# Self attention of a Perceiver layer: the two heads of a pair on row halves and column halves of TensorE, and the division moved ahead of the turn

## The chip, the cores and the metric

The kernel runs on one core of one Trainium2 chip. The metric is the device time of one execution in microseconds; the time before is the median of three runs, 806.36 us (806.20 to 808.21). All arithmetic is float32.

## The reference

One Perceiver layer for 256 query tokens of width 512. First comes a sigmoid cross attention over a context of 25088 rows, then self attention with 16 heads of width 64 that share one key and one value, then a mixture-of-experts feed-forward. The change touches the self attention alone:

```python
xn = layernorm(x)
q  = xn @ w_q.T                       # 16 heads of 64
k, v = split(xn @ w_kv.T)             # one key and one value, 64 wide, for all heads
sim  = (q * scale) @ k.T              # per head, 256 x 256, causal mask
attn = softmax(sim)                   # max, exp, sum, divide
out  = attn @ v                       # per head, 256 x 64
out  = layernorm(concat(out) @ w_out.T) * lno_g + lno_b
x    = x + out
```

## The kernel before

The 256 tokens stand as `NT` = 2 tiles of 128 (t = 0, 1); the 16 heads as `NE` = 8 pairs e, so that one pair has 128 channels, 64 of each head. The kernel goes through three stages in turn: the cross attention (49 groups of the context, about 560 us), the self attention, and the feed-forward. In the self attention nothing is loaded that isn't there yet; it is work of TensorE, VectorE, ScalarE and, in the new version, GpSimd, all of which run their instructions in order.

Before the pairs, `head_keys` and `head_values` make the shared key and value, and `queries(e)` (line 617) makes a pair's queries with four products of 256 columns. The key is kept in `kd` twice: rows 0 to 63 hold it in the first half of the columns, rows 64 to 127 in the second half, and the rest is zero. So one product with the full height of 128 rows (line 704) yields the scores of both heads of a tile t: 2 x 128 columns for t = 0 and 2 x 256 for t = 1, half of it multiplied by zeros.

For each tile t of a pair, `probabilities` adds the causal mask to the diagonal block (VectorE, line 707), takes the negated row maximum (line 709) and exponentiates head by head on ScalarE (line 712). `turned` transposes the probabilities on TensorE (line 727), six blocks of 128 x 128 per pair, and evicts them as `pT`. `weighted` multiplies each turned block as the stationary operand with `va` (line 751): the value with a column of ones as the 65th, so that the row sum comes out beside the weighted values. It divides with a reciprocal and a product on VectorE (lines 761 and 763). `outputs` turns the result (line 771) and evicts it to `oT` (line 777), from which `project` (line 677) makes the output, 2 x 8 products of 512 columns that add up in two PSUM banks.

The loop over e is a pipeline written by hand: in step e stand the queries of pair e+1, the turn of pair e-1, the scores of pair e, the values of pair e-1 and the outputs of pair e-2. Most of the pairs' instructions are placed by the scheduler from that order; the last pairs and everything marked `in_turn` stay as written. `fill` puts six of the projections between the last steps. PSUM has eight banks: six that rotate through `bank()`, so that the scores of consecutive tiles and pairs lie in different banks, and two that gather the projection.

Of the kernel before, what the change touches and what calls it, by code (L numbers as in the profile page):

```python
# [9 lines left out]
F32 = mybir.dt.float32  # L10
AF = mybir.ActivationFunctionType
ALU = mybir.AluOpType
AX = mybir.AxisListType

P = 128
# [6 lines left out]
def tile_perceiver_layer(  # L22
# [25 lines left out]
    nc = tc.nc  # L48

    T, D = x.shape  # L50
# [3 lines left out]
    DH = a_wkvT.shape[1] // 2  # L54
# [4 lines left out]
    NT = T // P  # L59
# [4 lines left out]
    NE = INNER // P  # L64
# [5 lines left out]
    small = ctx.enter_context(tc.tile_pool(name="small", bufs=4))  # L70
# [4 lines left out]
    psum = cross.enter_context(tc.tile_pool(name="psum", bufs=4, space=bass.MemoryType.PSUM))  # L75
    pacc = cross.enter_context(tc.tile_pool(name="pacc", bufs=4, space=bass.MemoryType.PSUM))

    def bank(name):
        return psum.tile([P, 512], F32, tag="ps", name=name)
# [72 lines left out]
    def all_of(src):  # L152
# [33 lines left out]
    ident = const.tile([P, P], F32, tag="ident", name="ident")  # L186
# [22 lines left out]
    tri = const.tile([P, 2, P], F32, tag="tri", name="tri")  # L209
# [6 lines left out]
        fill=NEG,  # L216
# [18 lines left out]
    in_turn = tc.keep_in_program_order  # L235
# [158 lines left out]
    sums, channel_sums = {}, {}  # L394
# [61 lines left out]
    for c in range(ND):  # L456
# [3 lines left out]
                lhsT=wqT_sb[:, c, :],  # L460
                rhs=xnT[:, c, :],
                start=(c == 0),
                stop=(c == ND - 1),
# [39 lines left out]
    for t in range(NT):  # L503
        for j in range(J):
# [4 lines left out]
                    rhs=ones_sb,  # L509
# [31 lines left out]
        layernorm(an[:, t, :], x1[:, t, :], f"a{t}", twice=True)  # L541

    cross.close()
    psum = ctx.enter_context(tc.tile_pool(name="psum_b", bufs=6, space=bass.MemoryType.PSUM))
    pacc = ctx.enter_context(tc.tile_pool(name="pacc_b", bufs=2, space=bass.MemoryType.PSUM))

# [54 lines left out]
    aq = hpool.tile([P, NE, T], F32, tag="aq", name="aq")  # L603
    oT = hpool.tile([P, NE, T], F32, tag="oT", name="oT")

    kd = hpool.tile([P, 2, T], F32, tag="kd", name="kd")
    nc.gpsimd.memset(kd, 0.0)

    va = hpool.tile([P, NT, DH + 1], F32, tag="va", name="va")
    nc.gpsimd.memset(va, 1.0)  # L610

    def queries(e, lo=0, hi=T, mark=lambda ins: ins):

        pa = bank(f"pa_{e}_{lo}")
        for c in range(ND):
            mark(
                nc.tensor.matmul(  # L617
                    pa[:, 0 : hi - lo],
                    lhsT=a_wqT_sb[:, c, e * P : (e + 1) * P],
                    rhs=anT[:, c, lo:hi],  # L620
                    start=(c == 0),
                    stop=(c == ND - 1),
                )
            )
        mark(
            nc.vector.tensor_scalar(aq[:, e, lo:hi], pa[:, 0 : hi - lo], 1.0 / DH, None, ALU.mult)
        )

    def head_keys(lo, hi):
        pkk = bank(f"pkk_{lo}")  # L630
        for c in range(ND):
            in_turn(
                nc.tensor.matmul(
                    pkk[:, 0 : hi - lo],
                    lhsT=a_wkv_sb[:, c, 0:2, :].rearrange("p i d -> p (i d)"),
                    rhs=anT[:, c, lo:hi],
                    start=(c == 0),
                    stop=(c == ND - 1),
                )
            )  # L640
        for i in range(2):
            nc.scalar.copy(
                kd[i * DH : (i + 1) * DH, i, lo:hi], pkk[i * DH : (i + 1) * DH, 0 : hi - lo]
            )

    def head_values(t):
        pv = bank(f"pv_{t}")
        for c in range(ND):
            in_turn(
                nc.tensor.matmul(  # L650
                    pv[:, :DH],
                    lhsT=anT[:, c, t * P : (t + 1) * P],
                    rhs=a_wkv_sb[:, c, 2, :],
                    start=(c == 0),
                    stop=(c == ND - 1),
                )
            )
        in_turn(nc.vector.tensor_copy(va[:, t, :DH], pv[:, :DH]))

    head_keys(0, P)  # L660
    queries(0, 0, P, in_turn)
# [13 lines left out]
    def project(t, e):  # L675
        in_turn(
            nc.tensor.matmul(  # L677
                pw[t],
                lhsT=oT[:, e, t * P : (t + 1) * P],
                rhs=a_wout_sb[:, e, :],  # L680
                start=(e == 0),
                stop=(e == NE - 1),
            )
        )

    fillers = [(0, e) for e in range(NE - 2)]

    def fill(e, n):
        for _ in range(n if e == NE - 1 else 0):
            project(*fillers.pop(0))  # L690

    def at_end(e, ins):
        if e >= NE - 1:
            in_turn(ins)

    def probabilities(e):

        found = []
        for t in range(NT):
            nk = (t + 1) * P  # L700
            nm = f"{e}_{t}"
            ps = bank(f"ps_{nm}")
            sc = ps[:, : 2 * nk].rearrange("p (i k) -> p i k", i=2)
            nc.tensor.matmul(  # L704
                sc, lhsT=aq[:, e, t * P : (t + 1) * P], rhs=kd[:, :, 0:nk], start=True, stop=True
            )
            nc.vector.tensor_add(sc[:, :, t * P : nk], sc[:, :, t * P : nk], tri)
            nmx = small.tile([P, 2], F32, tag="nmx", name=f"nmx_{nm}")
            nc.vector.tensor_reduce(nmx, sc, AX.X, ALU.max, negate=True)
            pe = work_b.tile([P, 2, nk], F32, tag=f"pe{t}", name=f"pe_{nm}")  # L710
            for i in range(2):
                nc.scalar.activation(pe[:, i, :], sc[:, i, :], AF.Exp, bias=nmx[:, i : i + 1])
            found.append(pe)
        return found

    def turned(e, found):

        done = []
        for t, pe in enumerate(found):
            fill(e, 2 - t)  # L720
            pt = bank(f"ptp_{e}_{t}")
            for kt in range(t + 1):
                for i in range(2):
                    o = (2 * kt + i) * P
                    at_end(
                        e,
                        nc.tensor.transpose(  # L727
                            pt[:, o : o + P], pe[:, i, kt * P : (kt + 1) * P], ident
                        ),
                    )  # L730
            n = 2 * (t + 1) * P
            pT = work_b.tile([P, n], F32, tag=f"pT{t}", name=f"pT_{e}_{t}")
            if t == 0:
                nc.scalar.copy(pT, pt[:, :n])
            else:
                nc.vector.tensor_copy(pT, pt[:, :n])
            done.append(pT)
        return done

    def weighted(e, done):  # L740

        fill(e, 2)
        po = bank(f"po_{e}")
        ov = po[:, : 2 * NT * (DH + 1)].rearrange("p (t i d) -> p t i d", t=NT, i=2)
        for t, pT in enumerate(done):
            for i in range(2):
                for kt in range(t + 1):
                    o = (2 * kt + i) * P
                    at_end(
                        e,  # L750
                        nc.tensor.matmul(  # L751
                            ov[:, t, i, :],
                            lhsT=pT[:, o : o + P],
                            rhs=va[:, kt, :],
                            start=(kt == 0),
                            stop=(kt == t),
                        ),
                    )
        rs = small.tile([P, NT * 2, 1], F32, tag="rsm", name=f"rsm_{e}")
        flat = ov.rearrange("p t i d -> p (t i) d")  # L760
        nc.vector.reciprocal(rs, flat[:, :, DH : DH + 1])
        on = work_b.tile([P, NT * 2, DH], F32, tag="oh", name=f"oh_{e}")
        nc.vector.tensor_mul(on, flat[:, :, 0:DH], rs.to_broadcast([P, NT * 2, DH]))
        return on

    def outputs(e, on):
        pt = bank(f"pto_{e}")
        for t in range(NT):
            at_end(
                e + 1,  # L770
                nc.tensor.transpose(
                    pt[:, t * P : (t + 1) * P],
                    on[:, 2 * t : 2 * t + 2, :].rearrange("p i d -> p (i d)"),
                    ident,
                ),
            )
        nc.scalar.copy(oT[:, e, :], pt[:, :T])

    found, heads = {}, {}
    for e in range(NE + 2):  # L780
        if e + 1 < NE:
            queries(e + 1)
        done = turned(e - 1, found.pop(e - 1)) if e - 1 in found else None
        if e < NE:
            found[e] = probabilities(e)
        if done is not None:
            heads[e - 1] = weighted(e - 1, done)
        if e - 2 in heads:
            if e == NE + 1:
                fill(NE - 1, len(fillers))  # L790
            outputs(e - 2, heads.pop(e - 2))


    fn = work.tile([P, NT, D], F32, tag="tok", name="fn")
# [16 lines left out]
        )  # L811
        layernorm(fn[:, t, :], x2[:, t, :], f"f{t}")

    project(0, NE - 2)
    project(1, 0)
    project(0, NE - 1)
    attended(0)
    for e in range(1, NE):
# [2 lines left out]
    attended(1)  # L821

    heads_end.close()
    few = ctx.enter_context(tc.tile_pool(name="few", bufs=1))


# [487 lines left out]
```

## Time and profile before

| What | Value |
|---|---|
| Median of 3 runs | 806.36 us (806.20 to 808.21) |
| The profiled execution: its own time, its span | 807.88 us, 805.8 us |
| Granted TensorE clock, mean over the span | 0.996 |
| Busy share: TensorE products (PE) | 98% |
| VectorE (DVE), ScalarE (ACT), GpSimd (POOL) | 62%, 13%, 1% |
| First product of scores, pair 0 | 586.08 us |
| First product of scores, pair 7 | 619.81 us |
| First transposition after the projection (`pt_fn`) | 639.07 us |
| Between the first and the last of these: busy TensorE, VectorE, ScalarE | 52.08, 30.65, 19.20 of 52.99 us |

Times inside the execution count from the start of the span. A float32 product is two matmul records in the trace (a transposition is one), and the columns that stream set its time: the 256-column records follow one another at 0.21 us, the 512-column ones at 0.43 us. The end of a record lies about 0.17 us behind the start of the one that follows, since the array is a pipeline. PE is TensorE's products, PEld its weight loads.

### The profile page before, as it was taken

The page shows a single profiled execution, that of the slowest core. Times are in us where ns is not written, and L with a number is a line of the kernel's source. Part 1 is how long each engine was busy: PE and PEld are TensorE (multiplying, and loading weights), DVE is VectorE, ACT ScalarE, POOL GpSimd, SP SyncE. Part 2 cuts the span into 40 slices and gives each one's busy share as a digit, 9 for nine tenths or more (in the row PEclk, how much of TensorE's full clock was granted, in tenths as well). Part 3 has the DMA queues.
Part 4 walks back from the last instruction along what each step waited for, and adds up shares of the span by engine and source line. Part 5 has one row for each costly group of instructions (what it writes and reads, how often), then busy time and mean ns, then how long its engine had stood idle before and what let it go on. Part 6 is the DMA issues. An engine that isn't in the chain of part 4 may idle for free.

```text
span 805.8 us, 8698 instructions
## 1 busy us (share of the span) xinstructions
PE 792.4 (98%) x3326; PEld 576.6 (72%) x3326; DVE 500.9 (62%) x828; ACT 108.6 (13%) x209; POOL 6.9 (1%) x28
## 2 busy tenths in 40 slices
PE   8999999999999999999999999999999999999996
PEld 5777777777777777777777777777687676776563
DVE  5766777667776677766777667776466563512212
ACT  2111110111001110011100111001234220110110
POOL 1000000000000000000000000000100000000000
PEclk9999999999999999999999999999999999999999
DMA  9997999999999888998889988810700032669500
GB/s 253 244 196 182 258 232 267 239 222 222 218 210 204 188 187 169 194 201 189 184 171 194 201 187 186 166 44 0 235 1 1 1 129 81 240 234 389 180 1 30
DMA packets 150495, 139.58 MB, mean 173 GB/s; under 512 B 7984, under 2 KB 109872, under 8 KB 150448
## 3 DMA queue, kind: packets, MB, share of 16 engines
q1 hardware_dynamic: 150160, 138.96, 73.0%
q8 instruction: 28, 0.46, 0.3%
q14 instruction: 19, 0.16, 0.1%
q10 hardware_dynamic: 288, 0.00, 0.0%
HBM read 138.42 MB, written 0.52 MB: 172 GB/s over the span
## 4 chain that ended last, share of the span: by engine, by line
PE 97%; DVE 1%; DMA 0%; ACT 0%; issue 0%; POOL 0%; POOLq 0%
PE xacc L439 37%; PE pk L338 21%; PE pz L360 11%; PE ph_e L873 7%; PE pd_e L919 3%; PE ph_s L873 3%; PE pa L617 2%; PE pw L677 2%; PE pd_s L919 2%; PE ph_few L1141 1%; PE ps L704 1%; PE po L751 1%; PE ph_first L873 1%; PE po_few L1172 1%; PE ptp L727 1%; PE py L530 1%
## 5 line engine op out<-in xcount | busy, mean ns | idle before, releaser
L338 PE MATMUL pk<-cT,wkT_sb 128*128 128x512 f32 x376 | 169.0, 592 | 0.0
L439 PE MATMUL xacc<-T,S 128*128 128x256 f32 x588 | 134.9, 379 | 0.0
L368 ACT ACTIVATE zT<-pz 128x512 f32<-128x512 f32 x98 | 58.3, 597 | 479.9 <-PE pz L360 479.2
L439 PEld LDWEIGHTS xacc<-T,S 128*128 128x128 f32 x588 | 111.7, 190 | 15.2
L338 PEld LDWEIGHTS pk<-cT,wkT_sb 128*128 128x128 f32 x376 | 71.4, 190 | 69.9 <-issue 67.4
L309 DVE STREAM_TRANSPOSE cT<-quarters 128x2048 f32<-128x2048 f32 x47 | 108.3, 2304 | 0.0
L439 PEld LDWEIGHTS xacc<-ctx,zT 128*128 128x128 f32 x392 | 74.3, 190 | 31.3 <-issue 23.0
L439 PE MATMUL xacc<-ctx,zT 128*128 128x256 f32 x392 | 93.0, 380 | 0.1
L360 PE MATMUL pz<-qT,kT 128*128 128x256 f32 x392 | 92.6, 379 | 0.0
L360 PEld LDWEIGHTS pz<-qT,kT 128*128 128x128 f32 x392 | 74.4, 190 | 10.1
L407 DVE TENSOR_TENSOR S<-zT 128x256 f32<-128x256 f32 x49 | 20.8, 425 | 91.5 <-ACT zT L368 91.5
L347 DVE TENSOR_SCALAR kT<-pk,bk 128x512 f32<-128x512 f32 x49 | 36.8, 750 | 59.8 <-PE pk L338 59.8
L873 PE MATMUL ph_e<-fT,gu 128*128 128x256 f32 x256 | 57.2, 381 | 0.0
L380 DVE TENSOR_TENSOR zsum<-zsum,zT 128x1024 f32<-128x1024 f32 x48 | 56.8, 1183 | 0.0
L873 PEld LDWEIGHTS ph_e<-fT,gu 128*128 128x128 f32 x256 | 48.1, 190 | 10.6 <-issue 3.8
L439 PE MATMUL xacc<-ctx,S 128*128 128x256 f32 x196 | 50.3, 379 | 0.0
L439 PE MATMUL xacc<-T,zT 128*128 128x256 f32 x196 | 50.3, 379 | 0.0
L439 PEld LDWEIGHTS xacc<-ctx,S 128*128 128x128 f32 x196 | 37.2, 190 | 5.1
L439 PEld LDWEIGHTS xacc<-T,zT 128*128 128x128 f32 x196 | 37.2, 190 | 5.1
L418 DVE TENSOR_TENSOR T<-ctx,T 128x512 f32<-128x512 f32 x49 | 33.9, 692 | 1.7
L419 DVE TENSOR_TENSOR T<-ctx 128x512 f32<-128x512 f32 x49 | 33.5, 685 | 0.0
L420 DVE TENSOR_TENSOR T<-T,ctx 128x512 f32<-128x512 f32 x49 | 33.5, 684 | 0.0
(228 smaller groups left out, 618.2 us busy)
## 6 DMA issues: line engine op xcount, KB each, us to landing
ctx<-in_context SPq DMA_DIRECT2D x48, 1024.0 KB, 6.9
quarters<-in_context SPq DMA_DIRECT2D x188, 256.0 KB, 9.2
gu<-in_e_gate_up SPq DMA_DIRECT2D x12, 1024.0 KB, 7.7
dn<-in_e_down SPq DMA_DIRECT2D x11, 512.0 KB, 6.2
gu_s<-in_s_gate_up SPq DMA_DIRECT2D x8, 512.0 KB, 5.9
a_wqT<-in_a_wqT SPq DMA_DIRECT2D x1, 2048.0 KB, 9.1
a_wout<-in_a_woutT SPq DMA_DIRECT2D x1, 2048.0 KB, 8.9
dn_s<-in_s_down SPq DMA_DIRECT2D x4, 512.0 KB, 7.6
```

The lines of the kernel that those rows point to most:

```text
L309: in_turn(nc.vector.transpose(cT, q.rearrange("p b (c r) -> p c b r", r=R)))
L338: nc.tensor.matmul(pk, lhsT=w[:, c, :], rhs=cT[:, c, :, :].rearrange("p b r -> p (b r)"), start=(c == 0), stop=(c == ND - 1),)
L347: in_turn(nc.vector.tensor_scalar(kT, pk, bk_sb, None, ALU.add))
L360: nc.tensor.matmul(pz[:, i * T : (i + 1) * T], lhsT=kT[:, j * P : (j + 1) * P], rhs=qT, start=True, stop=True,)
L368: nc.scalar.activation(zT[:, 2 * h : 2 * h + 2, :].rearrange("p j t -> p (j t)"), pz, AF.Sigmoid, scale=1.0 / math.sqrt(QK),)
L380: in_turn(nc.vector.tensor_add(zsum, zsum, zT))
L418: in_turn(nc.vector.tensor_sub(t2, c_of(ct, 1, 1), t1))
L419: in_turn(nc.vector.tensor_sub(t3, c_of(ct, 1, 1), c_of(ct, 0, 1)))
L420: in_turn(nc.vector.tensor_sub(t4, t2, c_of(ct, 1, 0)))
L439: nc.tensor.matmul(product[nm], lhsT=lhs[:, p, :], rhs=rhs[:, p, :], start=(g == 0 and p == 0 and nm in ("00", "2", "1", "11")), stop=(g = ...
L873: nc.tensor.matmul(ph[:, f * T + lo : f * T + hi], lhsT=gu[:, c, col : col + P], rhs=fT[:, c, lo:hi], start=(c == 0), stop=(c == ND - 1),)
L919: nc.tensor.matmul(pd, lhsT=hT[:, f, t * P : (t + 1) * P], rhs=dn[:, f, :], start=(f == 0), stop=(f == NI - 1),)
```

## The change

The scores: instead of one full-height product per tile, each head has its own product over 64 rows, head 0 on rows 0 to 63 and head 1 on rows 64 to 127, written to different PSUM banks. The tile of scores is now one object of two banks, `ps2`, with a single buffer (`bufs=1`): both tiles t of a pair lie in it, and the next pair's scores use it again. The rotating pool shrinks from six banks to four.

The softmax: the row sums come from the exponential itself (`accum_out`) instead of the column of ones. `divided` takes the reciprocal on VectorE and multiplies the probabilities on GpSimd, before they are turned. The turn of pair e-2 stands in step e now (it was pair e-1).

The values: the value is the stationary operand (128 rows x 64 columns) and the turned probabilities stream; head 0 writes PSUM partitions 0 to 63 and head 1 partitions 64 to 127. The result comes out turned already, so `outputs` with its transposition goes away, and so do the division on VectorE and the zeroed and doubled key `kd`.

The queries are evicted by ScalarE instead of VectorE, and one of the two turned blocks is evicted by the other engine than before. All instructions of the pairs now stay in program order.

```diff
-    psum = ctx.enter_context(tc.tile_pool(name="psum_b", bufs=6, space=bass.MemoryType.PSUM))
+    psum = heads_psum.enter_context(
+        tc.tile_pool(name="psum_b", bufs=4, space=bass.MemoryType.PSUM)
...
-        mark(
-            nc.vector.tensor_scalar(aq[:, e, lo:hi], pa[:, 0 : hi - lo], 1.0 / DH, None, ALU.mult)
+        in_turn(
+            nc.scalar.activation(aq[:, e, lo:hi], pa[:, 0 : hi - lo], AF.Copy, scale=1.0 / DH)
...
+    def scored(e):
+        ps = psum.tile([P, 2, 512], F32, tag="ps2", name=f"ps_{e}", bufs=1)
+        parts, maxima = [], []
+        for t in range(NT):
+            nk = (t + 1) * P
+            lo = t * P
+            parts.append(ps[:, :, lo : lo + nk])
+            for i in range(2):
+                half = slice(i * DH, (i + 1) * DH)
+                in_turn(nc.tensor.matmul(ps[:, i, lo : lo + nk],
+                        lhsT=aq[half, e, t * P : (t + 1) * P],
+                        rhs=kk[half, 0:nk], start=True, stop=True))
+        for t, sc in enumerate(parts):
+            diagonal = sc[:, :, t * P : (t + 1) * P]
+            in_turn(nc.vector.tensor_add(diagonal, diagonal, tri))
+            nmx = small.tile([P, 2], F32, tag="nmx", name=f"nmx_{e}_{t}")
+            in_turn(nc.vector.tensor_reduce(nmx, sc, AX.X, ALU.max, negate=True))
+            maxima.append(nmx)
+        return parts, maxima, []
+
+    def exponential(e, t):
...
+        for i in range(2):
+            in_turn(nc.scalar.activation(
+                    pe[:, i, :], parts[t][:, i, :], AF.Exp, bias=maxima[t][:, i : i + 1],
+                    accum_out=sums[:, i, :]))
+
+    def divided(e, t):
+        pe, sums = scores_of[e][2][t]
+        rs = small.tile([P, 2, 1], F32, tag="rsm", name=f"rsm_{e}_{t}")
+        in_turn(nc.vector.reciprocal(rs, sums))
+        nc.gpsimd.tensor_mul(pe, pe, rs.to_broadcast([P, 2, (t + 1) * P]))
...
+    def weighted(e, done):
+        po = bank(f"po_{e}")
+        for kt, pT in enumerate(done):
+            for i in range(2):
+                in_turn(nc.tensor.matmul(po[i * DH : (i + 1) * DH, kt * P : T],
+                        lhsT=va[:, kt, :], rhs=pT[:, i, :],
+                        start=(kt == 0), stop=(kt == NT - 1)))
+        in_turn(nc.scalar.copy(oT[:, e, :], po[:, :T]))
...
+    for e in range(NE + 2):
+        done = None
+        if e >= NE:
+            fill(2)
+        if e - 1 in scores_of:
+            divided(e - 1, 0)
+        if e - 2 in scores_of:
+            done = turned(e - 2)
+        if e - 1 in scores_of:
+            divided(e - 1, 1)
+        if e + 1 < NE:
+            queries(e + 1, mark=in_turn)
+        if e < NE:
+            scores_of[e] = scored(e)
+            exponential(e, 0)
+        else:
+            fill(1)
+        if done is not None:
+            weighted(e - 2, done)
+        if e < NE:
+            exponential(e, 1)
```

More of the change, by code (lines that the diff above doesn't have):

```diff
@@ L543, in tile_perceiver_layer @@
     cross.close()
-    psum = ctx.enter_context(tc.tile_pool(name="psum_b", bufs=6, space=bass.MemoryType.PSUM))
     pacc = ctx.enter_context(tc.tile_pool(name="pacc_b", bufs=2, space=bass.MemoryType.PSUM))
+    heads_psum = ExitStack()
+    psum = heads_psum.enter_context(
+        tc.tile_pool(name="psum_b", bufs=4, space=bass.MemoryType.PSUM)
+    )
     NS = IS // I
@@ L604, in tile_perceiver_layer @@
     oT = hpool.tile([P, NE, T], F32, tag="oT", name="oT")
[L606 to L610, printed above, removed]
+    kk = hpool.tile([P, T], F32, tag="kk", name="kk")
+    va = hpool.tile([P, NT, DH], F32, tag="va", name="va")
     def queries(e, lo=0, hi=T, mark=lambda ins: ins):
@@ L640, in head_keys @@
             )
[L641 to L644, printed above, removed]
+        nc.scalar.copy(kk[:, lo:hi], pkk[:, 0 : hi - lo])
     def head_values(t):
@@ L657, in head_values @@
             )
-        in_turn(nc.vector.tensor_copy(va[:, t, :DH], pv[:, :DH]))
+        in_turn(nc.vector.tensor_copy(va[:, t, :], pv[:, :DH]))
     head_keys(0, P)
@@ L684, in project, with fill @@
         )
-    fillers = [(0, e) for e in range(NE - 2)]
-    def fill(e, n):
-        for _ in range(n if e == NE - 1 else 0):
+    fillers = [(0, e) for e in range(NE - 1)] + [(1, 0)]
+    def fill(n):
+        for _ in range(n):
             project(*fillers.pop(0))
[L692 to L698, printed above, removed]
+    def scored(e):
+        ps = psum.tile([P, 2, 512], F32, tag="ps2", name=f"ps_{e}", bufs=1)
+        parts, maxima = [], []
@@ L699, in probabilities @@
         for t in range(NT):
             nk = (t + 1) * P
[L701 to L705, printed above, removed]
-            )
-            nc.vector.tensor_add(sc[:, :, t * P : nk], sc[:, :, t * P : nk], tri)
-            nmx = small.tile([P, 2], F32, tag="nmx", name=f"nmx_{nm}")
-            nc.vector.tensor_reduce(nmx, sc, AX.X, ALU.max, negate=True)
@@ L710, in probabilities @@
-            pe = work_b.tile([P, 2, nk], F32, tag=f"pe{t}", name=f"pe_{nm}")
-            for i in range(2):
[L712 to L726, printed above, removed]
+            lo = t * P
@@ new lines, in scored @@
+            parts.append(ps[:, :, lo : lo + nk])
+            for i in range(2):
+                half = slice(i * DH, (i + 1) * DH)
+                in_turn(
+                    nc.tensor.matmul(
+                        ps[:, i, lo : lo + nk],
+                        lhsT=aq[half, e, t * P : (t + 1) * P],
+                        rhs=kk[half, 0:nk],
+                        start=True,
+                        stop=True,
+                    )
+                )
+        for t, sc in enumerate(parts):
[4 more added lines that the diff above has]
+            maxima.append(nmx)
@@ new lines, in scored @@
+        return parts, maxima, []
+    def exponential(e, t):
+        parts, maxima, found = scores_of[e]
+        nm = f"{e}_{t}"
+        pe = work_b.tile([P, 2, (t + 1) * P], F32, tag=f"pe{t}", name=f"pe_{nm}", bufs=3)
+        sums = small.tile([P, 2, 1], F32, tag="sums", name=f"sums_{nm}")
+        for i in range(2):
+            in_turn(
+                nc.scalar.activation(
+                    pe[:, i, :], parts[t][:, i, :], AF.Exp, bias=maxima[t][:, i : i + 1],
+                    accum_out=sums[:, i, :],
+                )
+            )
+        found.append((pe, sums))
@@ new lines, in divided, with turned @@
+    def divided(e, t):
[3 more added lines that the diff above has]
+        nc.gpsimd.tensor_mul(pe, pe, rs.to_broadcast([P, 2, (t + 1) * P]))
+    def turned(e):
+        found = [pe for pe, _ in scores_of.pop(e)[2]]
+        done = []
+        for kt in range(NT):
+            pt = bank(f"ptp_{e}_{kt}")
+            n = (NT - kt) * P
+            for i in range(2):
+                for t in range(kt, NT):
+                    o = i * n + (t - kt) * P
+                    in_turn(
@@ L727, in turned @@
                         nc.tensor.transpose(
-                            pt[:, o : o + P], pe[:, i, kt * P : (kt + 1) * P], ident
-                        ),
-                    )
[L731 to L734, printed above, removed]
+                            pt[:, o : o + P], found[t][:, i, kt * P : (kt + 1) * P], ident
+                        )
+                    )
@@ L735, in turned @@
+            pT = work_b.tile([P, 2, n], F32, tag=f"pT{kt}", name=f"pT_{e}_{kt}")
+            to = pT.rearrange("p i q -> p (i q)")
+            if kt == 0:
+                in_turn(nc.vector.tensor_copy(to, pt[:, : 2 * n]))
             else:
-                nc.vector.tensor_copy(pT, pt[:, :n])
+                in_turn(nc.scalar.copy(to, pt[:, : 2 * n]))
             done.append(pT)
@@ L740, in weighted @@
     def weighted(e, done):
-        fill(e, 2)
         po = bank(f"po_{e}")
-        ov = po[:, : 2 * NT * (DH + 1)].rearrange("p (t i d) -> p t i d", t=NT, i=2)
-        for t, pT in enumerate(done):
+        for kt, pT in enumerate(done):
             for i in range(2):
[L747 to L757, printed above, removed]
-                    )
@@ L759, in weighted @@
[L759 to L777, printed above, removed]
@@ L779, in tile_perceiver_layer @@
-    found, heads = {}, {}
-    for e in range(NE + 2):
+                in_turn(
+                    nc.tensor.matmul(
+                        po[i * DH : (i + 1) * DH, kt * P : T],
+                        lhsT=va[:, kt, :],
+                        rhs=pT[:, i, :],
+                        start=(kt == 0),
+                        stop=(kt == NT - 1),
+                    )
+                )
+        in_turn(nc.scalar.copy(oT[:, e, :], po[:, :T]))
+    scores_of = {}
+    for e in range(NE + 2):
+        done = None
[7 more added lines that the diff above has]
+            divided(e - 1, 1)
@@ L781, in tile_perceiver_layer @@
         if e + 1 < NE:
-            queries(e + 1)
-        done = turned(e - 1, found.pop(e - 1)) if e - 1 in found else None
+            queries(e + 1, mark=in_turn)
         if e < NE:
-            found[e] = probabilities(e)
+            scores_of[e] = scored(e)
+            exponential(e, 0)
+        else:
+            fill(1)
         if done is not None:
[L787 to L791, printed above, removed]
+            weighted(e - 2, done)
@@ L812, in attended @@
         layernorm(fn[:, t, :], x2[:, t, :], f"f{t}")
-    project(0, NE - 2)
-    project(1, 0)
+    fill(len(fillers))
     project(0, NE - 1)
@@ L823, in tile_perceiver_layer @@
     heads_end.close()
+    heads_psum.close()
+    psum = ctx.enter_context(tc.tile_pool(name="psum_c", bufs=6, space=bass.MemoryType.PSUM))
     few = ctx.enter_context(tc.tile_pool(name="few", bufs=1))
```

## The prediction

> **What bounds the kernel now.** I read the chain of waits first, for the whole span and then in the middle of the self attention; then the timelines of VectorE and ScalarE for the same pairs, since the change moves work to them.
>
> ```profile
> PE 97%; DVE 1%; DMA 0%; ACT 0%; issue 0%; POOL 0%; POOLq 0%
> ```
>
> ```profile
> 597.77 1.73 PE pa L617 x8
> 599.50 0.66 PE ptp L727 x6
> 600.15 1.29 PE ps L704 x4
> 601.44 1.28 PE po L751 x12
> 602.73 0.22 PE pto L771 x2
> 602.95 1.73 PE pa L617 x8
> ```
>
> Columns: start, us, what. A pair takes 5.18 us (597.77 to 602.95), all of it TensorE: queries 1.73, turn 0.66, scores 1.29, values 1.28, turn of the result 0.22. No other engine is waited for. The first scores start at 586.08, those of pair 7 at 619.81 (33.73 us for seven steps: early pairs have less to do), and the stage ends 19.26 us later, at 639.07.
>
> ```profile
> 586.71 0.43 DVE L707 TENSOR_TENSOR ps<-ps,tri 128x256 f32<-128x256 f32 x1
> 587.18 0.42 DVE L709 TENSOR_REDUCE nmx<-ps 128x2 f32<-128x256 f32 x1
> 587.57 0.43 DVE L707 TENSOR_TENSOR ps<-ps,tri 128x256 f32<-128x256 f32 x1
> 588.04 0.69 DVE L709 TENSOR_REDUCE nmx<-ps 128x2 f32<-128x512 f32 x1
> ```
>
> ```profile
> 583.31 1.28 ACT L712 ACT_TABLE_LOAD   x1
> 587.64 0.63 ACT L712 ACTIVATE pe<-ps,nmx 128x128 f32<-128x128 f32 x2 [3.04 <-DVE nmx L709]
> 588.76 0.84 ACT L712 ACTIVATE pe<-ps,nmx 128x256 f32<-128x256 f32 x2 [0.50 <-DVE nmx L709]
> ```
>
> Mask and maximum of a pair take 2.1 us of VectorE, its exponentials 1.5 of ScalarE. Today this path is hidden: six PSUM banks rotate, so TensorE goes on with another pair meanwhile. The load of the exponential's table is done at 584.59, 3 us before it is needed.
>
> **What the change takes from TensorE.** Two products on different column tiles do run side by side on this chip; the routing stage shows it, four tiles of 32 columns each:
>
> ```profile
> 746.15 0.38 PE L1160 MATMUL pt_few<-ident,hf 128*128 128x128 f32 x2
> 746.47 0.63 PE L1141 MATMUL ph_few<-gu,fTf 128*32 128x512 f32 x3
> 746.49 0.62 PE L1141 MATMUL ph_few<-wvT,fTf 128*32 128x512 f32 x1
> 746.92 0.61 PE L1141 MATMUL ph_few<-gu,fTf 128*32 128x512 f32 x3
> ```
>
> Four records of 512 columns in 0.45 us, where one alone takes 0.43. Row halves are in no row; I take them to work alike. Scores: 128 + 256 columns per head, the heads side by side: 384 x 2 records' worth at 0.43 per 512 = 0.64 us (serial 1.29). Values: again 384 columns, 0.64 instead of 1.28. The turn of the result, 0.22, goes. Each change between whole array and tiles costs about 0.1 (746.15 + 2 x 0.11 = 746.37, next start 746.47); three per pair. TensorE's own need becomes 1.73 + 0.66 + 0.64 + 0.64 + 0.3 = 3.97 instead of 5.18.
>
> **What it adds: a ring.** The tile of scores has one buffer, so the first product of pair e+1 waits for the last exponential of pair e. In the changed kernel's instruction order with its waits, the first mask waits for the last of the four products, the first exponential for the second maximum, and on ScalarE the eviction `oT` stands between the exponentials of t = 0 and t = 1. Nothing overlaps inside the ring. One round:
> - scores 0.64; end of the last record and handover 0.21 (two 256-column records from 586.08, the mask at 586.71: 0.63 less 0.42);
> - mask, maximum, mask, maximum, each to the next start: 0.47 + 0.46 + 0.47 + 0.72 = 2.12 (588.04 to 588.76 is the last, with the handover to ScalarE);
> - exponentials of t = 0, pitch 0.27 each (0.63 less 0.36): 0.54; `oT` 0.28 (pitch 618.55 to 618.82 of two copies); exponentials of t = 1: 0.37 + 0.47: together 1.66;
> - back to TensorE 0.05 (its transposition started at 619.65 on an exponential that had ended at 619.60).
>
> Sum 4.68. Then the row sums: the built instruction stream has, behind each of the 16 x 2 exponentials, an instruction that reads the accumulator, a kind the old kernel lacks. The trace doesn't show one; the smallest ScalarE row is
>
> ```profile
> 650.79 0.29 ACT L909 ACTIVATE wsh<-lg 128x1 f32<-128x1 f32 x2
> 650.99 0.58 ACT L893 ACTIVATE hT_s<-ph_first 128x512 f32<-128x512 f32 x1
> ```
>
> pitch 0.10, alone 0.19. Pipelined a read costs 0.10; if it waits for the exponential in front to drain, 0.19 plus that exponential's lost overlap (0.36 less 0.27), 0.28; nothing only if it is hidden whole. I take 0.19, since a read of a sum can't begin before the last element is in: 4 x 0.19 = 0.76. The ring is 5.44 (4.68 to 5.80), more than TensorE's 3.97: the bound moves from TensorE to a chain of three engines. Seven rounds, less 0.28 twice (no `oT` in the first two), plus the table load: in the new order it stands behind a wait for the second maximum, so its 1.28 is bare: 38.08 - 0.56 + 1.28 = 38.80 instead of 33.73: **+5.07**.
>
> The Trainium skill ("TensorEngine Tiling (Array Packing)", PSUM Bottleneck) says that tiling speeds up TensorE but not the eviction of PSUM, which may become the bottleneck; it speaks against this change: by TensorE's rows alone the sum would be 8 x 1.21 = -9.7, by the ring it is +5.07 ahead of the tail.
>
> **The tail.** After pair 7's scores: scores 0.64, values of three pairs 1.92, two turns 1.31, sixteen projections at 0.853 = 13.65, six changes of tiling 0.6; the eviction of a turned block of pair 6 queues on ScalarE behind pair 7's last exponential, about 0.3. Sum 18.42 instead of 19.26: **-0.84**. GpSimd's product for pair 7 ends about 5.4 + 0.3 + 1.27 = 7.0 behind its scores; TensorE has work up to 7.4, so it is hidden, by 0.4.
>
> **GpSimd.** One product of 512 columns cost 1.27 (`xb`, L672), one of 256 lies between half of that and all of it. It starts when the next round does and holds up the turn at 1.55 of a round; queries end by 4. Cover 1.4; each us beyond would come seven times.
> **Priced at nothing:** the queries' eviction on ScalarE and the reciprocals on VectorE lie in the other engine's share of the ring (ScalarE waits some 2.9 us a round, VectorE 3); the dropped memsets of `kd` had long been done.
>
> **The clock.** TensorE now idles. The granted clock fell once before the attention:
>
> ```profile
> 566.00:567.00 1.00, 1.00 (x12) 1.00 (x11) 0.35 (x2) 0.00 (x0) 0.00 (x0) 1.00 0.00 0
> 568.00:569.00 1.00, 1.00 (x2) 0.46 (x2) 1.00 (x2) 0.00 (x0) 0.23 (x2) 0.50 0.46 88
> 570.00:571.00 1.00, 1.00 (x2) 0.33 (x1) 0.00 (x0) 0.00 (x0) 0.00 (x0) 0.50 1.08 379
> 571.00:572.00 1.00, 1.00 (x3) 0.38 (x2) 0.00 (x0) 0.00 (x0) 0.00 (x0) 0.96 1.17 332
> ```
>
> (The clock is the third last column.) From about 563.9 to 567.2 TensorE had only transpositions and one-column products, and then ran at 0.50 for some 3.2 us, losing 1.6. The gap of 1.65 us at 576.5 did not do it. In the new version nothing but transpositions runs for 4.1 us before pair 1's scores (ring 6.4 with the table load, less scores and queries 2.37) and for as long before pair 7's (5.44 less 1.28). Each could halve the clock for one such stretch, 0 to 1.6; most of the first hides in the ring: I take 0.9 for both, **+0.9**.
>
> The skill ("TensorE: Matmul & The Clock Gate", Part 1, The HAM clock gate) puts it so: an idle window of 3.4 us, free-running, halves the clock. The row agrees in length and factor; by the page a gap of 4.1 holds a whole window only one time in five, which would make it +0.3 and the sum +4.5.
>
> **Sum.** 5.07 - 0.84 + 0.9 = +5.1 us on the profiled execution (807.88 to 813.0); it ran 1.5 above the median, and the same difference on the median gives **811.5 us**.
>
> **Rivals.**
> 1. *The reads are free* (hidden whole behind the exponentials): ring 4.68, -0.25 - 0.84, plus 0 to 0.9 of clock: 805.3 to 806.2, no change. For it: exponentials overlap now. Against: a separate instruction in an in-order queue.
> 2. *Faster: TensorE stays the bound.* Place: the ring against TensorE's 3.97. Were the round below that, six rounds at 3.97, a last one without queries (2.3) and about 1.6 of filling give 27.7 between the scores instead of 33.7, with the tail -6.8: 799.6. It decides at a ring of 4.5: below it the kernel is faster by over 0.3%. That needs 0.2 less than my sum without any read, as if masks or exponentials overlapped; the waits speak against it.
> 3. *Row halves don't run side by side* (the change doesn't do what it says): scores 1.29, ring 6.1, +0.65 seven times and once in the tail: 816.7. The two heads write different banks, which speaks for their overlap; only column tiles are in the trace.
> 4. *GpSimd's product with a broadcast operand is slow*, up to three times `xb`, and holds turn, queries and so the next scores: at 3.7 instead of 1.27, one us more per round, 818.
>
> **How the numbers follow.** About 0.3% (2.4 us) is what a measurement here can tell from no change. Forecast 0.57, with reads from 0.10 to 0.28 (ring 5.08 to 5.80, -2.5 to +2.5) and clock 0 to 2.5: 808 to 816. Rivals: 0.16, 0.07, 0.12, 0.08. Faster is rival 2: 0.07. Same is rival 1 and the edge of the forecast: 0.18. Slower is the rest, 0.75. Leaving out rival 2 and the upper half of 3 and 4: 805 to 817.
>
> **What would show it.** Right: pair 1 to 7's scores start 5.1 to 5.8 apart and wait for ScalarE's exponentials; TensorE's busy time in the stage falls by 9 to 12 us while its length grows; 32 small ScalarE instructions; the table load right in front of the first exponential, behind the maxima; clock 0.5 somewhere near 593 or 625. Wrong: scores that end on the queries (TensorE still the bound), records of the two heads one behind the other, or a turn that waits for GpSimd in every round.

## The result, and the profile after

The changed kernel takes 811.84 us (median of four runs, 811.39 to 813.57) against 806.39 us of the kernel before in the same series: a ratio of 1.0066, with an interval of 1.0046 to 1.0087. It is slower by 5.45 us; the prediction said 811.5.

The profiled execution took 811.39 us with a span of 809.6. From pair 0's first scores to the first `pt_fn` (the stage, from here on) it needs 58.19 us instead of 52.99: **+5.20**. Of this +4.01 lies ahead of pair 7's scores and +1.19 behind them. The span grew by only 3.8, because this execution reached the stage 1.38 us earlier: the stretch of halved clock that the execution of before had at 567.7 is missing in it. That stretch comes and goes between executions of one kernel and moves single runs by some 1.5 us, so below the lengths of the stage are compared first. Behind `pt_fn` nothing changed (166.73 us, 166.75 before).

The chain of waits for the whole span, which was 97% TensorE:

```profile
PE 94%; DVE 2%; ACT 2%; DMA 0%; issue 0%; POOL 0%; ACTq 0%
```

The same chain in the middle of the stage (start, us, what):

```profile
601.56 0.95 PE ps L701 x8
602.53 0.45 DVE ps L711
603.00 0.44 DVE nmx L713
603.46 0.44 DVE ps L711
603.92 0.70 DVE nmx L713
...
604.73 0.15 ACT pe L724
...
605.54 0.26 ACT oT L778
605.80 0.93 ACT pe L724 x4
...
606.78 0.95 PE ps L701 x8
```

Before, a round of this chain was TensorE from end to end, 5.18 us. Now it is a ring of 5.22 us through three engines: scores and handover 0.97, masks and maxima up to the first exponential 2.20, exponentials of t = 0 with their reads 0.70, `oT` 0.25, exponentials of t = 1 with theirs 1.06, and 0.04 back to TensorE. The starts of the pairs' scores lie 6.20, 5.43 and then five times 5.22 us apart.

TensorE's timeline (start, us, engine, line, tile, shapes, records, and in brackets the idle time ahead with its releaser) shows that it is no longer the bound, and more:

```profile
592.83 3.58 PE L618 MATMUL pa<-anT,a_wqT 128*128 128x256 f32 x8
...
606.78 0.93 PE L701 MATMUL ps<-kk,aq 64*128 64x128 f32 x8 [0.96 <-ACT pe L724]
...
622.44 0.93 PE L701 MATMUL ps<-kk,aq 64*128 64x128 f32 x8 [2.69 <-ACT pe L724]
623.30 1.34 PE L770 MATMUL po<-pT,va 128*64 128x256 f32 x8
624.56 3.16 PE L675 MATMUL pw<-a_wout,oT 128*128 128x512 f32 x4
```

Ahead of the scores of pairs 3 to 6 it stands idle for 0.96 us each, until ScalarE's last exponential frees the tile of scores, and ahead of pair 7, where no queries are left to make, for 2.69. Its busy time in the stage fell from 52.08 to 48.17 while the stage grew. The queries at 592.83 take 3.58 us instead of 1.89, and four records of the projection at 624.56 take 3.16 instead of 1.98. The table by stretches (busy time of PE, PEld, DVE, ACT and POOL; the granted clock is the third last column) has the reason:

```profile
594.00:595.00 1.00, 1.00 (x4) 0.73 (x4) 0.10 (x2) 0.94 (x5) 0.00 (x0) 0.50 0.00 0
624.00:625.00 1.00, 1.00 (x7) 0.67 (x4) 0.93 (x3) 0.00 (x0) 0.00 (x0) 0.50 0.00 0
```

The clock is halved for 3.4 us from 592.8 and again from 623.6, once behind each long gap of TensorE. Last, ScalarE's timeline: the load of the table, bare behind a wait of 2.64 us, and the new instruction behind an exponential.

```profile
587.84 1.28 ACT L724 ACT_TABLE_LOAD   x1 [2.64 <-DVE nmx L713]
...
604.73 0.37 ACT L724 ACTIVATE pe<-ps,nmx 128x128 f32<-128x128 f32 x1 [2.68 <-DVE nmx L713]
605.00 0.19 ACT L724 ACTIVATION_READ_ACCUMULATOR pe<-ps,nmx 128x1 f32 x1
605.09 0.36 ACT L724 ACTIVATE pe<-ps,nmx 128x128 f32<-128x128 f32 x1
```

### The profile page after: what moved, and what is told of

The parts are those of the page before. It is cut to its first block, busy times and chain, and to the rows that moved or that the text cites. A ratio compares the mean times of both kernels' runs of the same rounds, so it can differ in the third digit from the quotient of the medians.

```text
span 809.6 us, 8738 instructions
## 1 busy us (share of the span) xinstructions
PE 787.5 (97%) x3310; PEld 567.3 (70%) x3310; DVE 497.1 (61%) x819; ACT 112.0 (14%) x248; POOL 19.4 (2%) x42
## 4 chain that ended last, share of the span: by engine, by line
PE 94%; DVE 2%; ACT 2%; DMA 0%; issue 0%; POOL 0%; ACTq 0%
PE xacc L439 36%; PE pk L338 21%; PE pz L360 10%; PE ph_e L884 7%; PE pd_e L930 3%; PE ph_s L884 3%; PE pw L675 2%; PE pd_s L930 2%; PE ph_few L1152 1%; ACT pe L724 1%; PE ph_first L884 1%; PE py L530 1%; PE pa L618 1%; DVE nmx L713 1%; PE ps L701 1%; DVE ps L711 1%
```

## Experiments

The theory: the single tile `ps2` ties scores, masks, exponentials and reads into one ring, and the ring sets the pace; what lies in it counts seven times, the table load once, and the idle time that it leaves brings the halved clock. The rivals: TensorE's own work sets the pace; the two heads gain nothing by running side by side; GpSimd's product holds up the turn. All diffs are against the changed kernel but the last, which shows what differs from the run before it; they leave out lines at the marks. Lengths of the stage are from one profiled execution each; 58.19 is the value to hold them against.

**The row sums without the reads.** The exponentials give no sums; the division goes by a constant 256, so this run's softmax is not normalised.

```diff
-        sums = small.tile([P, 2, 1], F32, tag="sums", name=f"sums_{nm}")
+        sums = flat_sums
...
-                    accum_out=sums[:, i, :],
...
+    flat_sums = hpool.tile([P, 2, 1], F32, tag="flat_sums", name="flat_sums")
+    nc.vector.memset(flat_sums, 256.0)
```

> Leaves out the row sums: the exponentials no longer add them up, and the division is by a constant 256 kept in a tile. Theory (the ring of scores, masks and exponentials through one tile of scores is the bound): in the changed kernel each read of the sums adds 0.09 us of pitch, four per round, so a round goes from 5.22 to 4.86 us, seven times, -2.5 us: about 809.3 us instead of 811.8. Rival (TensorE's own instructions and its changes of tiling are the bound): rounds stay at 5.22 and the time at 811.8, since nothing of TensorE changes. Second rival (the reads wait for the exponential to drain and cost 0.19 or more): -5 us.

Measured: 810.97 us (808.81 to 811.22), 1.0041 of before (1.0024 to 1.0058); the stage 56.08, -2.11. A round is 4.91 instead of 5.22. ScalarE's timeline has the two exponentials of t = 0 in one piece:

```profile
605.39 0.63 ACT L724 ACTIVATE pe<-ps,nmx 128x128 f32<-128x128 f32 x2 [2.73 <-DVE rsm L734]
605.91 0.37 ACT L777 COPY oT<-po 128x256 f32<-128x256 f32 x1
```

From the first exponential to `oT` it is 0.52 instead of 0.70: 0.09 a read. Four of them are the 0.31 that a round loses, to 0.08 each. What ScalarE saves, the whole ring saves: it sets the pace. The median fell by only 0.9 us, less than the 2.5 expected: this profiled execution, which is also the median one, has the stretch of halved clock at 568 that the one of after lacks.

**The table loaded early.** One exponential of a constant column ahead of the second half of pair 0's queries.

```diff
     head_keys(P, T)
+    warm_exp = small.tile([P, 1], F32, tag="warm_exp", name="warm_exp")
+    in_turn(nc.scalar.activation(warm_exp, eps_sb, AF.Exp))
     queries(0, P, T, in_turn)
```

> One exponential of a column of constants is put ahead of the second half of pair 0's queries on ScalarE, so that the table is loaded while TensorE still makes keys and queries. Theory: the bare 1.28 us between the second maximum and the first exponential goes; pair 0's to pair 1's scores fall from 6.21 to 4.93; the gap of TensorE in front of pair 1 falls from 3.35 to 2.1, so that the clock may stay at 1.0 there, for 0.5 more: -1.3 to -1.8 us, 810.0 to 810.5. Rival (something else holds pair 1 for as long): 811.8.

Measured: 811.31 us (808.91 to 813.10), 1.0042 (1.0025 to 1.0059). The stage is 56.50, -1.69: the first interval shrinks by 1.28, just the load, and the second by 0.34, since less of the halved clock now falls on the queries. The clock was halved all the same, at 591.9 and 622.7, though TensorE's gap ahead of pair 1 was now 2.07 us. The median follows only in part: this profiled execution has the stretch at 568 that the one of after lacks, and the runs scatter over both.

**Three idle products** of 512 columns ahead of the scores of pairs 1 and 7; their result is not used.

```diff
...
+        if e in (1, NE - 1):
+            warmed(f"pi_{e}", 3 if e == 1 else 3)
         if e < NE:
             scores_of[e] = scored(e)
```

> Three idle products of 512 columns on constants are added in front of the scores of pair 1 and three in front of those of pair 7, 2.56 us each, into a bank that nobody reads. Theory (the idle gap of 3.4 and the one of 2.7 us with a turn ahead of it halve the clock afterwards): the clock stays at 1.0 behind both, rounds stay at 5.22, the values and projections behind pair 7's scores go back to 0.85 and 1.9 us: -0.5 and -1.7, about 809.6. Rival (the halved clock comes from something else, as the low activity of tiled products): the clock still falls and the time stays at 811.8 or rises by up to 0.2 for the added products.

Measured: 810.18 us (808.95 to 811.18), 1.0040 (1.0029 to 1.0051); the stage 56.02, -2.17. The clock stays whole in it, and the first records of the projection behind pair 7 take their 1.98 again:

```profile
625.02 1.98 PE L675 MATMUL pw<-a_wout,oT 128*128 128x512 f32 x4
```

So filling the gaps keeps the clock, in this one profiled execution, and the two stretches cost 0.51 (the interval from pair 1 to 2, 4.92 instead of 5.43) and 1.65 (the tail, 18.80 instead of 20.45), together 2.16.

**The scores at full height**, side by side undone: the key twice, padded with zeros, each head over all 128 rows.

```diff
-    kk = hpool.tile([P, T], F32, tag="kk", name="kk")
+    kd = hpool.tile([P, 2, T], F32, tag="kd", name="kd")
+    nc.gpsimd.memset(kd, 0.0)
...
-                        lhsT=aq[half, e, t * P : (t + 1) * P],
-                        rhs=kk[half, 0:nk],
+                        lhsT=aq[:, e, t * P : (t + 1) * P],
+                        rhs=kd[:, i, 0:nk],
```

> Undoes the row halves alone: the key is kept twice with zeros again, and each head's scores are a product over all 128 rows, so that the heads follow one another; the single tile of scores and everything else stay. Theory (the scores stand in the ring): from the first score to the first mask 1.29 + 0.2 instead of 0.97, a round 5.22 + 0.5 = 5.7, seven times and once in the tail: +3.6 to +4.2 on the stage of 58.19 us, about 815.5. Rival (the heads on row halves save nothing because the ring is ScalarE and VectorE alone): 811.8.

Measured: 817.50 us (816.26 to 818.90), 1.0133 (1.0116 to 1.0150); the stage 62.66, +4.47.

```profile
602.81 1.58 PE L704 MATMUL ps<-kd,aq 128*128 128x128 f32 x8 [0.95 <-ACT pe L727]
```

The scores take 1.58 instead of 0.93 and the round 5.86 instead of 5.22: 0.64, all of it on the ring, the price that rival 3 of the prediction named. The median is 2 us above what was expected. In after the single records of the two heads start 7 ns apart (601.558 and 601.564, 601.771 and 601.778); here they follow one another.

**The values twice** for pairs 0 to 4, the second time over the first: more work for TensorE alone, off the ring.

```diff
-        for kt, pT in enumerate(done):
+        for kt, pT in [*enumerate(done)] * (2 if e <= NE - 4 else 1):
```

> The products with the values are made twice for pairs 0 to 4, which adds 0.7 us of TensorE to each of the rounds of pairs 2 to 6. Theory (TensorE waits 0.96 us in each round for the last exponential): the rounds stay at 5.22 and the time at 811.8, within 0.3 us; only the idle time falls, to about 0.25. Rival (TensorE's instructions pace the rounds): five rounds longer by 0.7, +3.5 us, 815.3.

Measured: 812.27 us (811.51 to 813.71), 1.0059 (1.0044 to 1.0075). The steady rounds stay at 5.21 to 5.22:

```profile
604.57 1.52 PE L770 MATMUL po<-pT,va 128*64 128x256 f32 x16
...
608.93 0.93 PE L701 MATMUL ps<-kk,aq 64*128 64x128 f32 x8 [0.31 <-ACT pe L724]
```

In these rounds TensorE works 0.65 us more and its wait falls by as much, from 0.96 to 0.31. Its own work does not set the pace. The stage grew by 0.59, which lies in the interval from pair 1 to 2 (6.11), where the clock was halved for 6.8 us instead of 3.4.

**Two tiles of scores.** Even pairs use the two banks in which the projection gathers later, as one tile for both of its halves.

```diff
...
-        ps = psum.tile([P, 2, 512], F32, tag="ps2", name=f"ps_{e}", bufs=1)
+        if e % 2:
+            ps = psum.tile([P, 2, 512], F32, tag="ps2", name=f"ps_{e}", bufs=1)
+        else:
+            ps = pair_psum.tile([P, 2, 512], F32, tag="two", name=f"ps_{e}")
...
+        if e == NE:
+            both = pair_psum.tile([P, 2, 512], F32, tag="two", name="pw_both")
+            pw.extend(both[:, t, :] for t in range(NT))
```

> Two tiles of scores in turn: even pairs use the two banks that later gather the projection, odd pairs the old tile. Nothing else moves. Theory (ring): the next scores no longer wait for the last exponential, but the next mask still does, since the reciprocal of the row sums stands ahead of it on VectorE. A round becomes reciprocal 0.2, masks and maxima 2.2, exponentials with reads and the eviction 2.0, handovers 0.05: 4.45 instead of 5.22, seven times -5 us, about 806 to 807. Rival (TensorE is the bound): no change, 811.8. If the rounds fall to 4.2, TensorE has taken over.

Measured: 809.38 us (808.36 to 810.73), 1.0028 (1.0013 to 1.0042); the stage 55.81, -2.38, half of the 5 us expected. The scores no longer wait for ScalarE, and the later rounds take 4.42 to 4.84. But from pair 1 to pair 2 it is 9.41 us:

```profile
590.86 0.48 PE L755 MATMUL ptp<-ident,pe 128*128 128x128 f32 x1 [2.48 <-POOL pe L741]
592.20 1.33 PE L755 MATMUL ptp<-ident,pe 128*128 128x128 f32 x5 [0.86 <-POOL pe L741]
593.32 3.62 PE L620 MATMUL pa<-anT,a_wqT 128*128 128x256 f32 x8
```

Without the ring GpSimd's product is late: by 2.48 and 0.86 us here, where the bare table load (still at 587.8) holds back the exponentials ahead of it, and by 0.26 and 0.42 in two later rounds. Over the gap the clock is halved (6.8 us from 590.7), and the queries behind it pay. The tail (22.49) has a wait of 1.79 us between the projection's halves, which now share one tile. The ring set the pace of the rounds; what it had hidden came to light.

**Two tiles, early table, queries ahead of the turn.** The version that follows from these: the second tile in a pool of its own that closes ahead of the projection, the early exponential, `queries(e + 1)` ahead of `turned(e - 2)` so that GpSimd has longer, and the projection spread anew between the last steps.

```diff
...
+    warm_exp = small.tile([P, 1], F32, tag="warm_exp", name="warm_exp")
+    in_turn(nc.scalar.activation(warm_exp, eps_sb, AF.Exp))
...
+        if e % 2:
+            ps = psum.tile([P, 2, 512], F32, tag="ps2", name=f"ps_{e}", bufs=1)
+        else:
+            ps = pair_psum.tile([P, 2, 512], F32, tag="two", name=f"ps_{e}")
...
-        if e >= NE:
+        if e == NE:
+            fill(3)
+        if e == NE + 1:
             fill(2)
         if e - 1 in scores_of:
             divided(e - 1, 0)
+        if e + 1 < NE:
+            queries(e + 1, mark=in_turn)
         if e - 2 in scores_of:
             done = turned(e - 2)
         if e - 1 in scores_of:
             divided(e - 1, 1)
-        if e + 1 < NE:
-            queries(e + 1, mark=in_turn)
...
+        if e == NE - 1:
+            pair_end.close()
+            pacc = heads_psum.enter_context(
+                tc.tile_pool(name="pacc_h", bufs=2, space=bass.MemoryType.PSUM))
+            pw.extend(accbank(f"pw_{t}") for t in range(NT))
...
-    for e in range(1, NE):
+    for e in range(AHEAD, NE):
         project(1, e)
```

> Puts together what the runs before gave: two tiles of scores in turn (the second in the banks of the projection, in a pool of its own that ends before the projection begins), the early table load, and in each step the queries of the next pair ahead of the turn, so that TensorE doesn't wait for GpSimd's product with the queries behind it; two more projections stand between the last steps. Theory: rounds of 4.45, set by reciprocal, masks and exponentials; no gap of TensorE over 2.5 us at the start, so at most one stretch of halved clock; first scores to the first transposition behind the projection 48 to 50 us instead of 58.19 and the old kernel's 52.99: 802 to 804 us, faster than both. Rival (with TensorE's instructions in this order another wait takes over at 5 us or more): 807 or above.

Measured: **803.35 us** (802.50 to 804.26), 0.9954 of the kernel before (0.9940 to 0.9967). It beats both.

```profile
596.97 0.93 PE L712 MATMUL ps<-kk,aq 64*128 64x128 f32 x8
597.82 0.92 PE L781 MATMUL po<-pT,va 128*64 128x256 f32 x8
598.67 1.99 PE L621 MATMUL pa<-anT,a_wqT 128*128 128x256 f32 x8
600.50 0.82 PE L761 MATMUL ptp<-ident,pe 128*128 128x128 f32 x6
601.25 0.93 PE L712 MATMUL ps<-kk,aq 64*128 64x128 f32 x8
```

In this round, from pair 3's scores to pair 4's, TensorE works without a gap, 0.85 + 0.85 + 1.83 + 0.75 = 4.28 us. But the step before took 5.46, and the next ones 4.42 and 4.36. The chain of waits shows why: from pair 0's masks to pair 7's exponentials it runs through VectorE and ScalarE alone.

```profile
602.23 0.17 DVE rsm L746
602.40 0.34 DVE ps L722
...
602.76 0.43 DVE nmx L724
...
603.69 0.70 DVE nmx L724
...
604.49 0.15 ACT pe L735
...
605.30 0.26 ACT oT L789
...
605.81 0.68 ACT pe L735 x3
...
606.58 0.17 DVE rsm L746
```

From one pair's second reciprocal to the next pair's it takes 4.35 to 4.42 us, near the 4.45 of the theory and some 0.8 less than a round before the change. TensorE's own 4.28 is just below it: the pace is still not TensorE's. The clock stays whole in the stage, which takes 48.44 us, 4.55 less than before. The work behind `pt_fn` took 167.77 us here, one more than in before and after. Of this 0.8 lies right behind `pt_fn`, where the first products of the gate (`pl`) wait longer, for VectorE's `rs_o`; the rest was not followed up.

**Both reciprocals between the masks.** In addition both reciprocals stand between the first maximum and the second mask of the next pair, so that the first mask no longer waits for the exponentials of the pair before. GpSimd's products start later for it.

```diff
             maxima.append(nmx)
+            if t == 0 and e - 1 in scores_of:
+                divided(e - 1, 0)
+                divided(e - 1, 1)
...
-        if e - 1 in scores_of:
+        if e >= NE and e - 1 in scores_of:
             divided(e - 1, 0)
+            divided(e - 1, 1)
...
-        if e - 1 in scores_of:
-            divided(e - 1, 1)
```

> As the run before, but both reciprocals of a pair stand between the masks of the next pair's first and second tile, so that masks no longer wait for the exponentials in front of them. Theory: the ring of VectorE and ScalarE is open, TensorE sets the round with 0.85 + 0.80 + 0.66 + 1.73 + 0.1 = 4.15 to 4.4; 1 us less than the run before, 801 to 803. Rival (GpSimd's product starts 2 us later in the round and holds the turn): rounds of 4.6 to 5, 803 to 806.

Measured: 805.36 us (803.61 to 807.02), 0.9986 (0.9975 to 0.9996), 2 us worse than without. The chain of waits is now TensorE's own, from pair 2's scores to pair 6's, as the theory had it:

```profile
595.48 0.72 PE ptp L764 x6
596.20 0.86 PE ps L712 x8
597.06 0.89 PE po L784 x8
597.94 1.92 PE pa L621 x8
599.87 0.71 PE ptp L764 x6
```

But its rounds, 4.38 to 4.44, are no shorter than those of the run before, and ahead of pair 7 the turn waits for GpSimd:

```profile
612.13 0.33 PE L764 MATMUL ptp<-ident,pe 128*128 128x128 f32 x1 [0.99 <-POOL pe L750]
613.13 0.89 PE L764 MATMUL ptp<-ident,pe 128*128 128x128 f32 x5 [0.67 <-POOL pe L750]
```

and the clock is halved behind that, from 613.6, and once more from 637.5 behind the stage. The stage takes 49.56, 1.1 more than in the run before; another 1.6 us lie in the 32 products `ph_first` under the second halved clock (5.42 instead of 3.79). Where no queries cover the turn, a reciprocal held back to the next pair's masks makes the product late.

## Why the prediction was right, step by step

- **The bound moves to a ring on one tile: right.** The chain names the predicted instructions in the predicted order, TensorE waits for ScalarE's exponentials, the round is 5.22 against 5.44, and the runs without reads, with doubled values and with two tiles each moved it as a ring would. Two terms were mis-sized. The scores with their handover take 0.97, not 0.85: the first two records of a head, of 128 columns, start 0.21 apart, where half of the 0.21 of 256 columns was reckoned. A read holds ScalarE for 0.08 to 0.09, not 0.19: its row is 0.19 to 0.22 long, but the next instruction begins beneath it. That was the choice between the bounds, and it was made wrongly: the value was below the lower of them, 0.10. Masks and maxima took 2.20 for 2.12, exponentials and `oT` less 0.09 a read 1.65 for 1.66. Net -0.22 a round, -1.5 for seven.
- **The table load bare, 1.28: right.** The early load took 1.28 from the first interval.
- **The tail, 18.42:** 18.80 with a whole clock (the run with the three added products). There pair 7's scores take 0.86, the values of three pairs 2.40 and the sixteen projections 14.24, each with its changes of tiling: 17.50, where the prediction had 0.64 + 1.92 + 13.65 + 0.6 = 16.81. The wait of 0.3 for an eviction did not come. +0.4.
- **The clock, +0.9:** the two places were right, 592.8 and 623.6, the price was 2.16, +1.3. That most of the first hides in the ring held (0.51). The step that failed is the one value of 0.9 for both: the second gap stands ahead of work with no idle time to hide in, so the whole price of a stretch, 1.65, comes out. The gaps were shorter than the 4.1 us of the prediction: 3.35 ahead of pair 1, and 2.69 behind a turn of 0.87 ahead of pair 7. By the Trainium skill ("TensorE: Matmul & The Clock Gate", Part 1, The HAM clock gate) an idle window of 3.4 us, free-running, halves the clock. The traces agree with the length, 3.41 us for each stretch and twice that for one, but not with the condition. The five profiled executions with this shape (after, no reads, early table, full height, doubled values) have ten such gaps of TensorE, 2.03 to 3.54 us long, and the clock was halved at nine of them; the one that it was not halved at is the longest, 3.54, ahead of pair 1 at full height. With the turn ahead of it counted as idle the second gap is 2.91 to 3.57. So less than a whole idle window was enough here; how much less, these runs don't show.
- **TensorE's busy time: a sign that missed.** In the stage it fell by 3.9 us, not by 9 to 12. The two stretches of halved clock add about 3.4 (estimate: half of 2 x 3.41, in which TensorE was busy throughout). The rest is TensorE's own need, which the prediction had at 3.97 a pair: in the last run, where TensorE sets the pace, it is 4.38 to 4.44.
- **The sum.** The errors, -1.5 + 0.4 + 1.3, come to +0.2 by these rounded figures on the predicted +5.1 in the stage; 5.20 was measured. That it came out so near is luck in the sizes: three errors that cancel, not three small ones.
- **The stepping from the profiled execution to the median** was right: the former lay 1.5 us above the latter, and of that 1.38 is the stretch at 567.7, ahead of the change.
- **The rivals.** *Reads free:* the reads were cheap but not free, and at 4.91 a round without them the kernel is still slower than before (1.0041). *TensorE stays the bound:* not so here, nor with two tiles alone or with the new order; only in the last run is it, at 4.38 to 4.44 a round and not at 3.97, since queries 1.92, turn 0.72, scores 0.86 and values 0.89, with the changes of tiling in them, come to 4.39. *Row halves not side by side:* they do run so, and undoing it costs 0.64 a round for the 0.65 that was named. *GpSimd slow:* its product of 512 columns took 1.04 us, less than `xb`'s 1.27. It was hidden, but only by the ring: without that it was late at once.

## What to carry to other kernels

When a change halves an engine's work, follow the tile that the work writes: with one buffer, the time from its first writer to its last reader is the pace, whatever the engines' own sums say. Price the idle time that a ring leaves as well, where it stands ahead of work that has no idle time of its own. And when a ring is taken out, look for what it had hidden: a table load, a product on a slow engine, the order of two steps and the banks of the projection lie here between 809.4 and 803.4 us, which one how much was not measured. Last, look at the chain again: the ring through TensorE was gone, and the one through VectorE and ScalarE that it had covered set the pace.

## What the runs showed of the hardware

- Products over rows 0 to 63 and rows 64 to 127, into different banks, start 7 ns apart and run side by side in float32; the eight records of a pair's scores take 0.93 us instead of 1.58.
- The sum of an exponential is an instruction of its own on ScalarE, 0.21 us long on average (32 of them, 6.6 us), of which 0.08 to 0.09 shows.
- Two waits of 0.99 and 0.67 us of TensorE, with a single transposition between them, were followed by 3.4 us of halved clock (the last kernel, 613.6). Before the change a wait of 1.65 us was not (578.1), nor was one of 0.95 ahead of 614.9 in the run before the last. Each of these is one execution; they give no threshold. Three products whose result nobody uses, 2.7 us of work, kept the clock whole in the profiled execution where the gap without them was 3.35 and 2.69.
- The product with an operand broadcast along the columns cost GpSimd 1.04 us for 512 columns and 0.61 for 256, less than the 1.27 of a sum of two full operands of 512.
